# Two units to a step in the first attention, with the order of every engine written out

## The chip, the cores and the metric

The kernel runs on one core of one Trainium2 chip. The core has a matrix engine (PE, with its weight loads PEld shown apart), a vector engine (DVE), an activation engine (ACT), a general engine (POOL) and DMA queues that SP issues. PE writes its products to PSUM, a small memory of eight banks; the other engines read them from there. The metric is the device time of one execution in microseconds; smaller is better. Several executions of a kernel are taken and their median is given; one more is taken with the hardware profiler.

## The reference

The input `x` is 8 batches of 512 rows of 256 numbers. Four blocks are added to it in turn, each on the layer-normalised rows: a first attention (8 heads of 64, keys and values from a shared latent of 64), a feed-forward stack of two layers with a local attention each, a second attention (16 heads of 16, causal), and the same feed-forward stack again. The change is in the first attention:

```python
q = (x @ Wq.T).reshape(b, t, N_HEADS, HEAD_DIM)
kv_latent = x @ Wkv_down.T
k = (kv_latent @ Wk_up.T).reshape(b, t, N_HEADS, HEAD_DIM)
v = (kv_latent @ Wv_up.T).reshape(b, t, N_HEADS, HEAD_DIM)
scores = jnp.einsum('bqhd,bkhd->bhqk', q, k) * HEAD_DIM ** (-0.5)
attn = jax.nn.softmax(scores, axis=-1)
out = jnp.einsum('bhqk,bkhd->bqhd', attn, v)
out = out.reshape(b, t, N_HEADS * HEAD_DIM) @ Wo.T
...
x = L0_attn_a_x
x = x + _L0_attn_a_ref(_layernorm(x, axis=-1), ...)
x = x + _L0_ffn_ref(_layernorm(x, axis=-1), ...)
x = x + _L0_attn_b_ref(_layernorm(x, axis=-1), ...)
x = x + _L0_ffn_ref(_layernorm(x, axis=-1), ...)
```

## The kernel before

Everything is in single precision. The eight batches go through in two groups of four; each group passes all stages, so the first attention (`attention_a`) runs twice. A batch's 512 rows are four row tiles (`i`) of 128. The key and value up-projections are folded into the query and output weights at the start of a group (`fold`), so that every head's scores are a product with the 64-wide latent.

A *unit* (L377) is one batch, one row tile and two of the eight heads (`u` from 0 to 3), so a row tile is four units and a batch sixteen. A unit is five parts:

- `scores` (L381): two products `s` of 64-row operands, which lie in two halves of the array (L389); DVE's maximum of both (`nm`, L393); ACT's two exponentials with row sums (`p`, shown at L241, a helper's line).
- `divide` (L402): DVE's reciprocal of the sums (L405), ACT's two scalings of `p` in place (L407).
- `turn` (L410): eight transposes of `p` on PE into PSUM (`ppt`, L414), DVE's copy to SBUF (`pt`, L416).
- `values` (L419): sixteen products for the weighted values, as 64-column operands in the two halves of the array, into `o` (L425). With the last unit of a row tile, ACT copies `o` to `oT` (L435).
- `project` (L438): only for the last unit of a row tile: four products `pp` (L443) and DVE's addition to the residual `x` (L444).

PSUM has three tiles of two banks (`ps_s`: `s` and `ppt` share them), one of one bank (`ps_mm`: `pp` and the pieces below) and one for `o` (`ps_o`). In SBUF `p` and `pt` have three buffers each.

`prologue` (L341) prepares a batch in pieces, one to each `yield`: the layer norm on DVE and POOL (`yr`), two rounds of transposes (`pyt`, L295) with ACT copies, the latent's product (`pd`, L354) with a DVE copy, its transposes (`pl`, L360) with an ACT copy, and four query products (`pq`, L370), each with an ACT copy into `qT` (L373).

`steps` takes one unit a step, software-pipelined: in step n unit n-1 is divided, unit n gets its scores, unit n-2 is turned, n-3 weighted and n-4 projected, and one piece of the next batch's prologue is placed behind the transposes. It gives only the order of the program's text; a scheduling layer below it orders the instructions of each engine, and moves independent ones past each other. Waits are put in where data or buffers ask for them. In the other attentions that freedom is taken away by `order_keeper` (L245), which chains all instructions of an engine in the order of the text. `EARLY_STEPS` (L32) lets the next stage's first two steps begin under the end of the stage before; the last steps of the stage call `ahead` to begin the next one.

The lines of `steps` that matter here:

```python
for part in (1, 0, 2, 3, 4):
    at = step - part
    if 0 <= at < len(units):
        got[at] = units[at][part](*got.get(at, ()))
    if part == 2:
        next(pieces, None)
if step > len(units) - 6:
    ahead[0]()
```

Of the kernel before, what the change touches and what calls it, by code (L numbers as in the profile page):

```python
# [17 lines left out]
P = 128  # L18
# [20 lines left out]
GELU_TABLES = "gelu_and_others"  # L39
Piece = namedtuple("Piece", "heavy first act second dve late", defaults=(None, None, None, None, None))  # L40
Unit = namedtuple("Unit", "n product inverse error refine masks squares masked highest exponentials turn keep_turned values project")
ISSUE_ORDER = mybir.DependencyInfo(mybir.DependencyClass.NoSync, mybir.DependencyReason.DATA)
WAIT = mybir.DependencyInfo(mybir.DependencyClass.Sync, mybir.DependencyReason.SCHED_ONLY)

# [2 lines left out]
def kernel(  # L47
# [259 lines left out]
    def attention_a(batches, g):  # L307
# [69 lines left out]
        def unit(b, i, u):  # L377

            n = f"a{b}_{i}_{u}"

            def scores():  # L381
                qT, latT, lat = state[b]
                if u == 0:
                    state["sums"] = pool.tile([P, H], F32, tag="sums", name=f"sums_{n}", bufs=3)
                sums = state["sums"]
                s = ps_s.tile([P, 2, T], F32, tag="s", name=f"s_{n}")
                for odd in range(2):
                    rows = slice(odd * HD, (odd + 1) * HD)
                    nc.tensor.matmul(  # L389
                        s[:, odd], lhsT=qT[rows, u, i * P : (i + 1) * P], rhs=latT[rows, :], start=True, stop=True  # L390
                    )
                nm = pool.tile([P, 2], F32, tag="nm", name=f"nm_{n}", bufs=4)
                nc.vector.tensor_reduce(nm, s, AX.X, ALU.max, negate=True)  # L393
                p = pool.tile([P, 2, T], F32, tag="p", name=f"p_{n}", bufs=3)
                for odd in range(2):
                    h = 2 * u + odd
                    function(
                        p[:, odd], s[:, odd], AF.Exp, bias=nm[:, odd : odd + 1], accum_out=sums[:, h : h + 1]
                    )
                return p, sums, lat  # L400

            def divide(p, sums, lat):  # L402

                some = sums[:, 2 * u : 2 * u + 2]
                nc.vector.reciprocal(some, some)  # L405
                for odd in range(2):
                    nc.scalar.activation(p[:, odd], p[:, odd], AF.Identity, scale=some[:, odd : odd + 1])  # L407
                return p, lat

            def turn(p, lat):  # L410
                ppt = ps_s.tile([P, 2, NT, P], F32, tag="s", name=f"ppt_{n}")
                for odd in range(2):
                    for k in range(NT):
                        nc.tensor.transpose(ppt[:, odd, k, :], p[:, odd, k * P : (k + 1) * P], ident)  # L414
                pt = pool.tile([P, 2, NT, P], F32, tag="pt", name=f"pt_{n}", bufs=3)
                nc.vector.tensor_copy(pt, ppt)  # L416
                return pt, lat

            def values(pt, lat):  # L419
                if u == 0:  # L420
                    state["o"] = ps_o.tile([P, 4, P], F32, tag="o", name=f"o_{n}")
                o = state["o"]
                for k in range(NT):
                    for odd in range(2):
                        nc.tensor.matmul(  # L425
                            o[odd * HD : (odd + 1) * HD, u, :],
                            lhsT=lat[:, k, :],
                            rhs=pt[:, odd, k, :],
                            start=(k == 0),
                            stop=(k == NT - 1),  # L430
                        )
                if u < 3:
                    return ()
                oT = pool.tile([P, 4, P], F32, tag="two", name=f"oT_{n}", bufs=5)
                nc.scalar.copy(oT, o)  # L435
                return (oT,)

            def project(oT=None):  # L438
                if oT is None:
                    return  # L440
                pp = ps_mm.tile([P, D], F32, tag="mm", name=f"pp_{n}")
                for k in range(4):
                    nc.tensor.matmul(pp, lhsT=oT[:, k, :], rhs=wvo_a[:, k, :], start=(k == 0), stop=(k == 3))  # L443
                nc.vector.tensor_add(xs[b][:, i, :], pp, xs[b][:, i, :])  # L444

            return scores, divide, turn, values, project

        units = [unit(b, i, u) for b in batches for i in range(NT) for u in range(4)]
        each = NT * 4
        def steps(ahead):  # L450
            tables_of(EXP_TABLES)
            got, pieces = {}, iter(())
            for step in range(len(units) + 4):
                if step % each == 2 and step // each + 1 < len(batches):
                    pieces = prologue(batches[step // each + 1])
                for part in (1, 0, 2, 3, 4):
                    at = step - part
                    if 0 <= at < len(units):
                        got[at] = units[at][part](*got.get(at, ()))
                    if part == 2:  # L460
                        next(pieces, None)
                if step > len(units) - 6:
                    ahead[0]()
                yield

# [3 lines left out]
        def head():  # L469
            yield from prologue(batches[0])  # L470
            while phase["gates"]:
                yield
            for _ in range(EARLY_STEPS):
                next(rest)
                yield

        def run(ahead):
            follower.append(ahead)
# [1121 lines left out]
```

## Time and profile before

| what | value |
|---|---|
| runs | 4411.23, 4412.81, 4419.76 us; median 4412.81 us |
| span of the profiled execution | 4418.4 us |
| busy: PE, DVE, ACT, POOL | 4201.7, 3082.6, 2700.4, 1148.4 us |
| first attention, first group | first score product at 26.3 us, last one at 287.1 us |
| first attention, second group | first score product at 2219.5 us, last one at 2484.3 us |
| `s` maximum (L393), 64 in a group | 1.22 us each |
| `pt` copy (L416), 64 in a group | 1.22 us each |
| exponential of 128x512 (L241) | 0.68 us each |
| scaling of 128x512 (L407) | 0.72 us each |

The profile comes from one execution, whose span stands beside the runs' median; it is some 6 us above it. "Busy" is the time in which an engine had an instruction under way. Successive instructions of an engine overlap a little, so a step is measured from start to start. A wait is shown as idle time of an engine and what ended it. The granted clock is the share of full clock that PE had.

### The profile page before, as it was taken

To read this page: it belongs to the slowest core of one execution; us is meant where nothing else is said; L and a number is where in the kernel's file an instruction comes from. 1 tells how busy PE (TensorE), PEld (TensorE's weight loads), DVE (VectorE), ACT (ScalarE), POOL (GpSimd) and SP (SyncE) were. 2 spreads that over 40 slices of the span, in tenths; PEclk is the share of its full clock that TensorE was granted. 3 is DMA by queue.
4 is the path that set the end of the run, shared out by engine and by line. 5 is a ranking of instruction groups with operands and counts; after the bars stand their busy time and mean duration, and the time that the engine had idled before them with its cause. 6 is when DMAs were issued, how large, how long until landed. Compare 5 with 4: busy or idle time off the path is not lost.

```text
span 4418.4 us, 70438 instructions
## 1 busy us (share of the span) xinstructions
PE 4201.7 (95%) x26580; PEld 2539.8 (57%) x26580; DVE 3082.6 (70%) x7497; ACT 2700.4 (61%) x6316; POOL 1148.4 (26%) x1140
## 2 busy tenths in 40 slices
PE   9999999999998899999999999999999988999999
PEld 5666556655555465566566665565545554655655
DVE  6678737747999886377466786377479997863773
ACT  6777517716998675176167675276179886742761
POOL 0014214312222342143200242243122223422431
PEclk9999999999999999999999999999999999999999
DMA  2000000000000000000100000000000000000000
GB/s 82 1 22 4 24 3 23 3 24 20 2 1 2 20 4 7 5 21 13 53 30 1 20 4 23 22 4 23 5 21 1 1 1 20 4 6 23 3 4 24
DMA packets 51091, 63.36 MB, mean 14 GB/s; under 512 B 6336, under 2 KB 45504, under 8 KB 50752
## 3 DMA queue, kind: packets, MB, share of 16 engines
q1 hardware_dynamic: 50752, 58.85, 4.1%
q8 instruction: 211, 3.46, 0.3%
q14 instruction: 128, 1.05, 0.1%
HBM read 46.28 MB, written 4.19 MB: 11 GB/s over the span
## 4 chain that ended last, share of the span: by engine, by line
PE 74%; DVE 13%; ACT 11%; issue 1%; POOL 1%; DMA 0%; SPq 0%; POOLq 0%; ACTq 0%; DVEq 0%
PE pu_g1x L932 3%; PE pu_g0x L932 3%; PE pu_g0y L932 3%; PE pu_g1y L932 3%; PE s_a L389 3%; PE o_a L425 3%; PE ppt_a L414 3%; PE pqk_f1x L510 2%; PE pqk_f1y L510 2%; PE pqk_f0y L510 2%; PE pqk_f0x L510 2%; ACT r_b L241 2%; PE ppt_b L1269 2%; DVE pt_b L1274 2%; ACT num_b L241 2%; DVE r_b L1220 2%
## 5 line engine op out<-in xcount | busy, mean ns | idle before, releaser
L1269 PE MATMUL ppt_b<-ident,num_b 128*128 128x128 f32 x1280 | 224.1, 293 | 88.0 <-DVE pt_b L1274 63.2
L1269 PEld LDWEIGHTS ppt_b<-ident,num_b 128*128 128x128 f32 x1280 | 138.5, 144 | 273.0 <-ACT num_b L241 98.0
L241 ACT ACTIVATE num_b<-num_b,most_b 128x512 f32<-128x512 f32 (+3 forms) x512 | 280.7, 552 | 21.8 <-POOL most_b L1249 21.4
L1274 DVE COPY pt_b<-ppt_b 128x512 f32<-128x512 f32 (+1 forms) x352 | 224.1, 637 | 33.3 <-PE ppt_b L1269 32.5
L241 ACT ACTIVATE p_a<-s_a,nm_a 128x512 f32<-128x512 f32 x256 | 173.7, 683 | 105.2 <-DVE nm_a L393 102.2
L1216 DVE TENSOR_TENSOR t_b<-den_b,r_b 128x1024 f32<-128x1024 f32 (+1 forms) x176 | 197.4, 1122 | 46.3 <-ACT r_b L241 45.7
L1239 DVE CUSTOM_DVE_ANT_0 num_b<-num_b,r_b 128x512 f32<-128x512 f32 (+3 forms) x512 | 223.9, 485 | 1.9 <-POOL num_b L1232 1.9
L1232 POOL TENSOR_TENSOR num_b<-num_b,causal 128x256 f32<-128x256 f32 (+2 forms) x176 | 174.2, 990 | 186.3 <-ACT num_b L1226 185.8
L1197 PE MATMUL den_b<-st_b,st_b 18*128 18x384 f32 (+3 forms) x1024 | 210.9, 476 | 0.4 <-ACT num_b L1226 0.4
L393 DVE TENSOR_REDUCE nm_a<-s_a 128x2 f32<-128x1024 f32 x128 | 156.4, 1223 | 70.4 <-PE s_a L389 70.4
L1220 DVE SCALAR_TENSOR_TENSOR r_b<-t_b,r_b 128x1024 f32<-128x1024 f32 (+1 forms) x176 | 204.6, 1163 | 0.2
L1197 PE MATMUL dot_b<-st_b,st_b 16*128 16x384 f32 (+3 forms) x1024 | 191.4, 475 | 5.5 <-ACT yT_b L1075 4.4
L241 ACT ACTIVATE p_f1y<-p_f1y,nm_f1y,rn_f1y 128x256 f32<-128x256 f32 (+1 forms) x256 | 143.8, 564 | 80.6 <-DVE nm_f1y L649 80.5
L241 ACT ACTIVATE p_f0y<-p_f0y,nm_f0y,rn_f0y 128x256 f32<-128x256 f32 (+1 forms) x256 | 143.7, 563 | 80.6 <-DVE nm_f0y L649 80.6
L241 ACT ACTIVATE p_f1x<-p_f1x,nm_f1x,rn_f1x 128x256 f32<-128x256 f32 (+1 forms) x256 | 143.8, 564 | 75.4 <-DVE nm_f1x L649 75.3
L241 ACT ACTIVATE p_f0x<-p_f0x,nm_f0x,rn_f0x 128x256 f32<-128x256 f32 (+1 forms) x256 | 143.8, 564 | 75.2 <-DVE nm_f0x L649 75.2
L407 ACT ACTIVATE p_a<-p_a,sums_a 128x512 f32<-128x512 f32 x256 | 172.0, 720 | 26.5 <-DVE sums_a L405 26.5
L241 ACT ACTIVATE r_b<-den_b 128x1024 f32<-128x1024 f32 (+1 forms) x176 | 165.9, 942 | 33.7 <-PE den_b L1197 16.3
L1226 ACT ACTIVATE num_b<-dot_b 128x1024 f32<-128x1024 f32 (+1 forms) x176 | 164.7, 936 | 28.2 <-PE dot_b L1197 27.9
L1249 POOL TENSOR_SCALAR most_b<-most_b 128x2 f32<-128x2 f32 (+2 forms) x176 | 34.2, 194 | 568.1 <-DVE most_b L1239 552.9
L241 ACT ACTIVATE r_b<-r_b 128x1024 f32<-128x1024 f32 (+1 forms) x176 | 172.5, 980 | 5.6
L552 POOL TENSOR_TENSOR ro_f0x<-ro_f0x,rs_f0x 128x512 f32<-128x512 f32 x64 | 80.3, 1276 | 360.5 <-DVE rs_f0x L541 144.8
(356 smaller groups left out, 11296.5 us busy)
## 6 DMA issues: line engine op xcount, KB each, us to landing
x<-in_x SPq DMA_DIRECT2D x8, 512.0 KB
out<-x SPq DMA_DIRECT2D x8, 512.0 KB
wf_0x<-in_f_wqkv SPq DMA_DIRECT2D x2, 1536.0 KB
wf_0y<-in_f_wqkv SPq DMA_DIRECT2D x2, 1536.0 KB
wf_1x<-in_f_wqkv SPq DMA_DIRECT2D x2, 1536.0 KB
wf_1y<-in_f_wqkv SPq DMA_DIRECT2D x2, 1536.0 KB
wg_0x<-in_f_w SPq DMA_DIRECT2D x2, 1386.0 KB
wg_0y<-in_f_w SPq DMA_DIRECT2D x2, 1386.0 KB
```

The lines of the kernel that those rows point to most:

```text
L241: i = nc.scalar.activation(out, in_, func, **more).ins
L407: nc.scalar.activation(p[:, odd], p[:, odd], AF.Identity, scale=some[:, odd : odd + 1])
L510: nc.tensor.matmul(dst.rearrange("p h d -> p (h d)"), lhsT=hTs[b][:, k, t * P : (t + 1) * P], rhs=wqkv[:, k, c * INNER : (c + 1) * INNER], ...
L932: nc.tensor.matmul(pu[: cols.stop - cols.start, c], lhsT=w1[:, k, cols], rhs=hT[:, k, :], start=(k == 0), stop=(k == 1),)
L1197: return nc.tensor.matmul(s[:, a, m * width : (m + 1) * width], lhsT=left[at, j, past:width], rhs=right[at, j, :width], start=True, stop=True,
L1216: nc.vector.tensor_mul(t[:, :, :cols], den[:, :, :cols], r[:, :, :cols])
L1220: nc.vector.scalar_tensor_tensor(r[:, :, :cols], t[:, :, :cols], 2.0, r[:, :, :cols], ALU.subtract, ALU.mult)
L1226: nc.scalar.activation(num[:, :, :cols], dot[:, :, :cols], AF.Square, scale=-0.5)
L1232: nc.gpsimd.tensor_add(own, own, mask)
L1239: nc.vector.tensor_tensor_reduce(out=s4[:, a, m, :], in0=s4[:, a, m, :], in1=r4[:, a, m, :], scale=-1.0, scalar=LOWEST, op0=ALU.mult, op1= ...
L1269: nc.tensor.transpose(ppt[:, k, :], p[:, a, k * P : (k + 1) * P], ident)
L1274: nc.vector.tensor_copy(pt[:, a, :nblocks, :], ppt[:, :nblocks, :])
```

## The change

One step takes a *pair* of units. Every part of a unit becomes a function of its own: `scores` is now only the products, then `maxima`, `exponentials`, `invert`, `divide`, `turn`, `keep_turned`, `values`, `keep_values`, `project` and `add`. `steps` writes out their order: the products of both new units, then the weighted values of both units of two steps ago, then the maxima of the new pair, the copy `oT` where a row tile is done, the exponentials of both, and then unit by unit the transposes of the pair of one step ago with their copies, the reciprocals and the scalings. A prologue piece stands between the two turns where a row tile is done, and at the step's end otherwise; the layer norm of the next batch stands at the end of a batch's first step. All this is under `order_keeper`, so that each engine keeps the order of the text. The head of the stage takes one step (one pair) early where it took two of one unit. No buffer count changes.

```diff
         units = [unit(b, i, u) for b in batches for i in range(NT) for u in range(4)]
-        each = NT * 4
+        pairs = [units[at : at + 2] for at in range(0, len(units), 2)]
+        each = NT * 2
+
         def steps(ahead):
             tables_of(EXP_TABLES)
-            got, pieces = {}, iter(())
-            for step in range(len(units) + 4):
-                if step % each == 2 and step // each + 1 < len(batches):
-                    pieces = prologue(batches[step // each + 1])
-                for part in (1, 0, 2, 3, 4):
-                    at = step - part
-                    if 0 <= at < len(units):
-                        got[at] = units[at][part](*got.get(at, ()))
-                    if part == 2:
+            kept_order = order_keeper()
+            pieces = iter(())
+
+            def pair(m):
+                return pairs[m] if 0 <= m < len(pairs) else ()
+
+            for m in range(len(pairs) + 2):
+                new, turning, weighted = pair(m), pair(m - 1), pair(m - 2)
+                done = weighted[1] if weighted and m % 2 else None
+                with kept_order():
+                    for some in new:
+                        some.scores()
+                    for some in weighted:
+                        some.values()
+                    for some in new:
+                        some.maxima()
+                    if done:
+                        done.keep_values()
+                    for some in new:
+                        some.exponentials()
+                    if turning:
+                        turning[0].turn()
+                        turning[0].keep_turned()
+                    if new:
+                        new[0].invert()
+                    if done:
                         next(pieces, None)
-                if step > len(units) - 6:
+                    if new:
+                        new[0].divide()
+                    if turning:
+                        turning[1].turn()
+                        turning[1].keep_turned()
+                    if new:
+                        new[1].invert()
+                        new[1].divide()
+                    if done:
+                        done.project()
+                        done.add()
+                    else:
+                        next(pieces, None)
+                    if m % each == 0 and m // each + 1 < len(batches):
+                        pieces = prologue(batches[m // each + 1])
+                        next(pieces)
+                if m > len(pairs) - 3:
+                    ahead[0]()
                     ahead[0]()
                 yield
...
-            for _ in range(EARLY_STEPS):
-                next(rest)
-                yield
+            next(rest)
+            yield
```

Inside `unit`, the parts are the same instructions as before, split into these functions; what a part hands to the next stands in a dictionary `got` of the unit.

## The prediction

> **What bounds the kernel now.** I read the page's busy shares first, then the chain that ended last, then the windows cut at the batches of the first attention, then TensorE's order of time inside one of them, and last the waits. A "quad" below is four units (one row tile), a "pair" two.
>
> Of the page, the first line shows the busiest engine, the second what the end of the span hangs on:
>
> ```profile
> PE 4201.7 (95%) x26580; PEld 2539.8 (57%) x26580; DVE 3082.6 (70%) x7497; ACT 2700.4 (61%) x6316; POOL 1148.4 (26%) x1140
> ...
> PE 74%; DVE 13%; ACT 11%; issue 1%; POOL 1%; DMA 0%; SPq 0%; POOLq 0%; ACTq 0%; DVEq 0%
> ```
>
> Both are averages over stages. The windows (start:end, length, then busy time of PE, PEld, DVE, ACT, POOL, then granted clock) show the first attention's second and third batch and three quads of its fourth, and below them a stretch of the second attention for the clock:
>
> ```profile
> 93.40:160.50 67.10, 67.10 (x513) 42.45 (x512) 47.24 (x69) 49.10 (x108) 1.46 (x3) 1.00 0.00 1
> 160.50:227.70 67.20, 67.20 (x515) 42.49 (x514) 43.71 (x57) 49.20 (x108) 1.21 (x2) 1.00 0.00 1
> 227.70:270.70 43.00, 43.00 (x361) 28.40 (x360) 31.54 (x39) 34.32 (x76) 0.00 (x0) 1.00 0.02 4
> 1300.00:1400.00 100.00, 92.03 (x828) 51.52 (x826) 90.34 (x196) 87.03 (x171) 21.51 (x40) 0.93 0.01 1
> ```
>
> In the first attention PE has no gap at all: other engines have a third to spare. So only fewer PE microseconds can shorten this stage, and any wait that PE gets lengthens it. One quad and the beginning of the next, in PE's order of time (start, length, instruction):
>
> ```profile
> 213.31 1.13 PE L389 MATMUL s_a<-latT_a,qT_a 64*128 64x512 f32 x4
> 214.37 1.09 PE L414 MATMUL ppt_a<-ident,p_a 128*128 128x128 f32 x8
> 215.39 1.09 PE L425 MATMUL o_a<-pt_a,lat_a 128*64 128x128 f32 x16
> 216.41 1.13 PE L389 MATMUL s_a<-latT_a,qT_a 64*128 64x512 f32 x4
> ...
> 225.73 1.99 PE L443 MATMUL pp_a<-wa,oT_a 128*128 128x256 f32 x8
> 227.66 1.13 PE L389 MATMUL s_a<-latT_a,qT_a 64*128 64x512 f32 x4
> ```
>
> From start to start: s 1.06, ppt 1.02, o 1.02, pp 1.93; a quad is 227.66 - 213.31 = 14.35 us. Elsewhere ppt takes 0.93 when a product of its own array shape follows (204.51 to 205.44, then pq), so each change of shape costs about 0.09 at the end of one, and two s in a row took
>
> ```profile
> 2219.47 1.99 PE L389 MATMUL s_a<-latT_a,qT_a 64*128 64x512 f32 x8
> 2221.29 0.38 PE L961 MATMUL po_g0y_mm<-wg_0y,gT_g0y 42*128 42x256 f32 x1
> ```
>
> 1.82 us against 2 x 1.06; with a change of shape behind them 1.91.
>
> **What the change saves on PE.** s,s 1.91 for 2.12; o,o and (where nothing comes between) ppt,ppt have no row: at most 2.04 (nothing saved), at least 1.86 (2 x 0.93); I take 1.90. Per pair 0.21 + 0.14 + 0.14 = 0.49, per quad 0.98, over 32 quads (two groups of four batches of four) 31 us. That would be the gain with PE still full. No product, transpose, DMA or ACT pass is added or dropped. EARLY_STEPS for this attention goes from two units to one pair, the same work.
>
> **What the fixed order adds.** Three PSUM buffers serve s, s, ppt, ppt. In the changed kernel's allocation, a step's first s takes the buffer of the step before's first ppt, its second s that of the second s before, its second ppt that of its own first s. So PE waits (1) at the first s for the copy pt of the first ppt one step back, (2) at the second ppt for the first unit's exponentials. Behind (1) everything on PE waits, behind (2) the projection too; neither was a wait before, since each unit's chain had a unit's time for itself. On ACT, in steps that finish a quad, the copy oT stands ahead of the exponentials, and so waits for the second o.
>
> Latencies, from rows: ppt's start to its copy's start 1.08 (299.07 to 300.15), copy 1.22, a DVE end to PE's start 0.14:
>
> ```profile
> 44.19 1.22 DVE L416 COPY pt_a<-ppt_a 128x1024 f32<-128x1024 f32 x1
> ...
> 45.55 0.52 PE L414 MATMUL ppt_a<-ident,p_a 128*128 128x128 f32 x3 [0.58 <-DVE pt_a L416]
> ```
>
> *Step without a finished quad*: s,s 0 to 1.91, o,o to 3.81, first ppt 3.81, its copy 4.89 to 6.11, next s at 6.25. PE alone would need 1.91 + 1.90 + 1.90 = 5.7: 0.55 of wait. (DVE is free at 3.3: two maxima of 1.12 from 1.06 on.)
>
> *Step with one*: second o starts at 2.78; o's start to oT's 1.14 (303.76 to 304.90): 3.92; oT holds ACT 0.47 (156.18 to 156.65); exponentials of unit one 4.39 to 5.85 (first one's start to the reciprocal's wait end, 148.63 to 150.11, less 0.03); second ppt 5.99, pp 6.92 (0.93), next s 8.7 (1.8: like pq 205.44 to 207.25). PE alone 5.7 + 1.8 = 7.5: 1.2 of wait.
>
> Together 14.95 for a quad against 14.35: **the two waits (1.75) eat the 0.98 and more, +0.6 per quad without other work.** With hand-overs between engines at nothing it would be 5.9 + 8.3 = 14.2 (0.87 of transposes, then the copy; ACT's two passes, then pp); with each of the six 0.1 longer, 15.55.
>
> **Where the next batch's preparation fills the waits.** It is eight pieces of PE work; before, they cost PE 67.1 - 4 x 14.35 = 9.7 us a batch. Afterwards: in a finishing step they lie between the two ppt, in the 1.2 us hole. pd (1.7) makes it 9.3, pq (its ACT copy must free the one mm buffer before pp) 9.65; in a plain step pyt and pl (0.4 to 0.6) hide wholly, pq gives 7.4 (5.55 + 1.71 + 0.1). Against that, two new stalls at a batch's start: the layer norm is in DVE's fixed order (statistics 1.75, 11.46 to 13.21; POOL 1.4 to 14.59; rows 1.38), ahead of the next maxima, and the last qT copy stands behind both divisions on ACT, so the second s waits 1.1. The step after it takes 11.1. Steps of one batch: 7.4, 11.1, 6.25, 9.3, 6.25, 9.65, 7.4, 9.65 = 67.0, against 67.1: no change in two of four batches.
>
> *First batch.* From its unit 4 on, 48.5 to unit 16 (6.25, 9.3, 6.25, 9.65, 7.4, 9.65), against 53.1 (40.3 to 93.4). But in the first group unit 4 starts later: maximum of unit 1 ends about 34.6, its exponentials 36.1, then on DVE the layer norm (4.6), a maximum (1.1), the rotation tables (2.77, which stood at 40.31 before) and a maximum, then the copy: s of unit 4 at 47.1 instead of 40.3. Net +2.2. In the second group the layer norm lies under the feed-forward's last products (2221 to 2231): unit 4 at 2236.9 for 2237.6, net -5.2.
>
> *Last batch.* Steps 7.4, 9.8, then 6.25 and 8.7 twice = 47.1 for 43.05: +4.05. The tail, to the end of the last pp, interleaved with the next stage's start: before 36.8 us (270.7 to 307.5); after 39.3, since two of pht, hT, pqk and of POOL's sum, pqt leave some 3 us of PE holes where 1.3 stood. +2.5.
>
> Sum: group one 2.2 - 0.2 + 4.05 + 2.5 = +8.5; group two -5.2 - 0.2 + 4.05 + 2.5 = +1.1; **+9.6 us on the profiled 4418.4 = 4428.0.** That execution lies 5.6 above the runs' median of 4412.81, so the runs should read about **4422.5**, +0.22%. The two groups' whole stage is some 560 us; the rest of the kernel keeps its order.
>
> What about the clock: it was granted 1.00 here and 0.93 in the stretch of the second attention above, where PE is 92% busy and turns much by transposes. In the new quads PE will be 89% busy (14.35 - 0.98 of 14.95), and between the last o and pp lie 3.3 us with only transposes. I take no loss from it; the rival below prices one.
>
> [...]
>
> **Rivals.**
> *PE stays full* (not slower): the waits are hidden because some hand-over is shorter or ACT runs ahead. It holds if the copy ends before 5.6 and the exponentials before 4.6 of their steps. For it: DVE and ACT are idle a third. Against it: both waits are chains of latency, not of load. 4412.8 - 31 = 4382; half hidden 4398 to 4402.
> *The clock drops* (slower than forecast): holes and transposes bring the 0.93 of that stretch here. On half of the stage's 560 us PE loses 280 x 0.07 = 20, of which the holes hide perhaps a quarter: 4437. For it: the stretch's busy share is like the new one. Against it: no window of this stage is under 1.00. It decides from a granted clock of 0.97 over the stage.
> *It does little, within 0.2%*: the same mechanism, with a per-quad price of +0.4 instead of +0.6, gives 32 x -0.2 = -6: 4416.
>
> **How the numbers follow.** My mechanism 0.65 (own range 4412 to 4434: per-quad error of 0.3 over 32 quads), two fifths of it inside 0.2% (8.8 us, about what a measurement of this kernel can tell from no change: 4404 to 4421.6), PE full or nearly 0.2, clock 0.15. Slower 0.65 x 0.6 + 0.13 = 0.52; faster 0.2; same 0.65 x 0.4 + 0.02 = 0.28. The range reaches down to half-hidden waits and up to the clock's case: 4396 to 4440, leaving about 0.12 below and 0.07 above.
>
> **What will show it.** Right: PE's idle before s_a put down to pt_a some 0.5 us in every second step, before ppt_a to the exponentials p_a about 1.2 in the others; starts of s pairs 6.25 and 8.7 apart in the last batch; s,s 1.91; a batch near 67. Wrong: s pairs at 5.7 and 7.5 (PE full), a granted clock under 1.00 in the windows, a layer norm that runs elsewhere on DVE, or a time shift in stages that the change does not touch.

## The result, and the profile after

| | before | after |
|---|---|---|
| median of 4 runs | 4414.36 us | 4432.69 us |
| ratio, 95% interval | | 1.004 [1.0026, 1.0054] |
| span of the profiled execution | 4418.4 us | 4430.5 us |
| first attention, group one | 288.63 us | 300.16 us |
| first attention, group two | 292.64 us | 296.01 us |
| PE busy in both groups | 574.6 us | 554.6 us |
| PE idle in both groups | 6.7 us | 41.6 us |

The changed kernel is 0.4% slower. The two stage lengths run from the first score product of a group to the first weighted values of the next stage, read from TensorE's order of time; from here on "the stages" are both together. They grew by 11.5 and 3.4, together 14.9 us; the medians differ by 18.3. Of the 14.9, PE's work fell by 20.0 us, and its idle time rose by 34.9.

The page's first line and its chain answer to the two shown of before:

```profile
PE 4175.9 (94%) x26580; PEld 2547.3 (57%) x26580; DVE 3073.0 (69%) x7497; ACT 2690.1 (61%) x6316; POOL 1147.7 (26%) x1140
...
PE 72%; DVE 14%; ACT 12%; issue 1%; POOL 1%; DMA 0%; SPq 0%; POOLq 0%; ACTq 0%; DVEq 0%
```

PE is busy 26 us less and the span is 12 us longer; two per cent of the chain went from PE to DVE and ACT. The windows of the changed kernel, cut at the second batch, the third batch, the hole at the start of group one and the end of the third batch's first finishing step (columns as before):

```profile
96.85:164.14 67.29, 64.07 (x513) 43.43 (x513) 44.67 (x65) 47.69 (x108) 1.20 (x2) 1.00 0.00 1
164.14:233.78 69.64, 65.51 (x513) 44.35 (x513) 48.73 (x85) 47.69 (x108) 3.75 (x7) 0.98 0.00 1
...
36.00:48.30 12.30, 4.11 (x22) 3.26 (x20) 9.65 (x26) 6.10 (x15) 1.21 (x2) 0.72 0.00 0
...
182.00:185.25 3.25, 3.05 (x9) 2.25 (x9) 2.42 (x7) 2.59 (x5) 0.00 (x0) 0.62 0.00 0
```

Before, the second batch took 67.10 us with PE busy for all of it. Now it takes 67.29 with PE busy for 64.07: three microseconds of work are saved and three of waiting put in their place. The third batch is 2.4 us longer than before, and in two places the granted clock is far under 1.00. One quad of the last batch, and the beginning of the next, in PE's order of time (L numbers are now lines of the changed kernel):

```profile
257.23 1.99 PE L393 MATMUL s_a<-latT_a,qT_a 64*128 64x512 f32 x8 [0.44 <-DVE pt_a L430]
259.15 1.97 PE L439 MATMUL o_a<-pt_a,lat_a 128*64 128x128 f32 x32
261.05 1.09 PE L426 MATMUL ppt_a<-ident,p_a 128*128 128x128 f32 x8
263.15 1.09 PE L426 MATMUL ppt_a<-ident,p_a 128*128 128x128 f32 x8 [1.01 <-ACT p_a L244]
264.08 1.89 PE L455 MATMUL pp_a<-wa,oT_a 128*128 128x256 f32 x8
265.90 1.99 PE L393 MATMUL s_a<-latT_a,qT_a 64*128 64x512 f32 x8
...
272.13 1.13 PE L393 MATMUL s_a<-latT_a,qT_a 64*128 64x512 f32 x4 [0.44 <-DVE pt_a L430]
```

From start to start, the scores of a pair (s,s) take 1.92 and its weighted values (o,o) 1.90; a finishing step, one in which a row tile's projection is done, takes 8.67 (257.23 to 265.90), a plain one 6.23 (265.90 to 272.13). The two waits stand where the prediction put them: 0.44 us at the first score product for the copy `pt`, 1.01 us at the second turn for the exponentials. Steps of the changed kernel, in microseconds from one pair's first score product to the next ("behind the layer norm", below also "layer norm step", is the step after the one at whose end the next batch's layer norm stands):

| step | forecast | measured |
|---|---|---|
| plain | 6.25 | 6.22 |
| finishing a quad | 8.7 | 8.67 |
| plain, with a query product | 7.4 | 7.43 |
| finishing, with `pd` | 9.3 | 9.34 |
| finishing, with a query product | 9.65 | 9.66 |
| behind the layer norm, second batch | 11.1 | 11.32, 11.33 |
| behind the layer norm, third batch | 11.1 | 13.68, 13.18 |
| a batch with pieces, second / third | 67.0 | 67.29, 67.30 / 69.64, 69.14 |
| start of unit 4 in group one | 47.1 | 48.31 (the stage began 0.94 later) |

### The profile page after: what moved, and what is told of

Same layout as the page of the kernel before. It is cut to its first block, busy times and chain, and to the rows that moved or that the text cites. A ratio compares the mean times of both kernels' runs of the same rounds, so it can differ in the third digit from the quotient of the medians.

```text
span 4430.5 us, 70536 instructions
## 1 busy us (share of the span) xinstructions
PE 4175.9 (94%) x26580; PEld 2547.3 (57%) x26580; DVE 3073.0 (69%) x7497; ACT 2690.1 (61%) x6316; POOL 1147.7 (26%) x1140
## 3 DMA queue, kind: packets, MB, share of 16 engines
q14 instruction: 128, 1.05, 0.1%
## 4 chain that ended last, share of the span: by engine, by line
PE 72%; DVE 14%; ACT 12%; issue 1%; POOL 1%; DMA 0%; SPq 0%; POOLq 0%; ACTq 0%; DVEq 0%
PE pu_g1x L983 3%; PE pu_g0x L983 3%; PE pu_g0y L983 3%; PE pu_g1y L983 3%; PE o_a L439 3%; PE s_a L393 3%; PE pqk_f0y L561 2%; PE pqk_f1y L561 2%; PE pqk_f0x L561 2%; PE pqk_f1x L561 2%; ACT r_b L244 2%; PE ppt_a L426 2%; PE ppt_b L1320 2%; DVE pt_b L1325 2%; ACT num_b L244 2%; DVE r_b L1271 2%
## 5 line engine op out<-in xcount | busy, mean ns | idle before, releaser
L244 ACT ACTIVATE num_b<-num_b,most_b 128x512 f32<-128x512 f32 (+3 forms) x512 | 280.7, 552 | 20.2 <-POOL most_b L1300 19.8
L430 DVE COPY pt_a<-ppt_a 128x1024 f32<-128x1024 f32 x128 | 155.7, 1219 | 106.3 <-PE ppt_a L426 106.3
L1277 ACT ACTIVATE num_b<-dot_b 128x1024 f32<-128x1024 f32 (+1 forms) x176 | 164.6, 935 | 27.7 <-PE dot_b L1248 27.6
L603 POOL TENSOR_TENSOR ro_f1x<-ro_f1x,rs_f1x 128x512 f32<-128x512 f32 x64 | 80.4, 1278 | 363.0 <-DVE rs_f1x L592 149.7
```

The lines of the kernel that those rows point to most:

```text
L244: i = nc.scalar.activation(out, in_, func, **more).ins
L430: nc.vector.tensor_copy(got["pt"], got.pop("ppt"))
L1277: nc.scalar.activation(num[:, :, :cols], dot[:, :, :cols], AF.Square, scale=-0.5)
```

## The experiments

Each version was timed beside the kernel before, whose medians were 4416.0, 4418.6 and 4415.1 us in the three series. "Stages" is the difference to before in the two stage lengths together, "PE" the difference in PE's busy time inside them, "idle" PE's idle time there, "half clock" the time inside them for which the record of the granted clock stands at 0.5; all are from the profiled execution. e3_between, e5_keep_later and e6_single_kept were executed five times, the other experiments eleven; the profiled execution of e3_between lies 11.6 us under its median and that of e2_ln_free 7.8 us, so for these two the stages and the medians need not agree.

| version | median us | ratio, interval | stages | PE | idle | half clock |
|---|---|---|---|---|---|---|
| before | | | 0 | 0 | 6.7 | 0 |
| changed | 4432.69 | 1.0040 [1.0026, 1.0054] | +14.9 | -20.0 | 41.6 | 13.7 |
| e1_free | 4417.53 | 1.0007 [0.9999, 1.0016] | +2.2 | -21.3 | 30.2 | 3.4 |
| e2_ln_free | 4425.97 | 1.0022 [1.0013, 1.0031] | +8.9 | -23.2 | 38.7 | 0 |
| e3_between | 4433.96 | 1.0039 [1.0024, 1.0054] | +12.4 | -12.8 | 31.8 | 20.5 |
| e4_both | 4407.42 | 0.9984 [0.9975, 0.9993] | -5.7 | -19.8 | 20.7 | 3.4 |
| e5_keep_later | 4438.04 | 1.0055 [1.0041, 1.0069] | +19.0 | -16.1 | 41.8 | 23.9 |
| e6_single_kept | 4457.18 | 1.0088 [1.0074, 1.0102] | +42.6 | +18.0 | 31.3 | 34.1 |
| e7_between_free | 4426.44 | 1.0015 [1.0007, 1.0024] | +10.7 | +3.9 | 13.4 | 0 |
| e8_more_p | 4420.37 | 1.0011 [1.0002, 1.0020] | +8.3 | -20.0 | 34.9 | 23.9 |
| e10_single_ln_free | 4416.94 | 1.0004 [0.9995, 1.0013] | +5.1 | +0.8 | 10.9 | 0 |
| e11_both_ahead | 4409.59 | 0.9989 [0.9980, 0.9998] | -9.8 | -20.5 | 17.4 | 0 |
| e12_ln_free_keep_between | 4404.48 | 0.9978 [0.9969, 0.9986] | -8.9 | -27.9 | 25.7 | 0 |
| e13_keep_between | 4421.35 | 1.0014 [1.0005, 1.0023] | +7.1 | -19.5 | 33.2 | 23.9 |

### What the fixed order costs: e1_free, e2_ln_free

```diff
-            kept_order = order_keeper()
+            kept_order = nullcontext
```

> The changed kernel without the fixed order: the text keeps its pairs, each engine's order is free. TensorE's order and the allocation of the three PSUM tiles stay those of pairs; what moves are the layer norm and some copies on DVE and ACT. Theory A (the hand-over of PSUM tiles inside a step sets the time, the layer norm in its fixed place adds to it): quads of the last batch stay near 14.9 us, the finishing step a little shorter if ACT takes oT later; the layer norm steps fall from 11.3 and 13.7 to about 9.3 us and the hole of 15 us at the start of group one shrinks by some 6 us; time 4405 to 4420. Theory B (the loss of freedom itself costs, pairs alone would gain): quads of 13.3 us or less and a time of 4382 to 4400.

The time is that of theory A, and theory B's falls: pairs without the fixed order are as fast as before, not faster. But a quad of the last batch takes 13.66 us, nearer to B's 13.3 than to A's 14.9, since the finishing step is 7.44: the free order puts `oT` behind the first unit's exponentials, between its two scalings, which A had down as "a little shorter". In exchange a finishing step with `pd` takes 10.1 to 10.9 us, and 15.2 in the first batch of group two; in the second batch PE is idle for 1.5 us of it before `pp_a`.

In e2_ln_free only the layer norm is outside:

```diff
-                    if m % each == 0 and m // each + 1 < len(batches):
-                        pieces = prologue(batches[m // each + 1])
-                        next(pieces)
+                if m % each == 0 and m // each + 1 < len(batches):
+                    pieces = prologue(batches[m // each + 1])
+                    next(pieces)
```

> The changed kernel, with only the next batch's layer norm taken out of the fixed order. Theory A: the plain and finishing steps stay 6.22 and 8.67 us; the steps of 11.3 (second batches) and 13.7 and 13.2 us (third batches) become about 9.3, and unit 4 of group one starts near 41 to 42 us instead of 48.3: 6.8 + 2 + 4.4 + 2 + 3.9 = 19 us less than the changed kernel, about 4414. Theory B' (the place of the layer norm costs nothing, another engine is late there): no change, 4430 to 4435.

Unit 4 of group one starts at 42.51 instead of 48.31, the layer norm steps of group one are 10.77 us instead of 11.32 and 13.68; plain and finishing steps stay 6.22 and 8.67. The direction is A's, the size a third of it: 6.0 us instead of 19. The steps don't come down to 9.3, because PE still waits three times in them: 0.84 us at the second score product for the last query copy, 0.58 at the second turn for the exponentials, and 0.72 at `pp_a`, which needs the PSUM tile of the transposed rows, whose copy stands on ACT behind the exponentials.

What "outside" means shows on DVE: the rows `yr` of the third batch are normalised from 50.5 to 53.0 us, and their first transpose follows at 105.2, so that nothing waits for them. It isn't free everywhere. The first batch of group one is 5.2 us shorter than in the changed kernel and the third batches 2.9 and 2.4, but the second batches are 0.7 us longer each (the step behind the layer norm step grows from 6.22 to 7.48; on DVE, rows of the next stage now stand between the maxima), and the first batch of group two is 3.2 us longer: there statistics of the layer norm stand ahead of a copy `pt` on DVE and wait 3.83 us for the transfer of `x`, and PE waits 2.45 us for that copy.

The third batch of the changed kernel shows why the layer norm is dearer there. Its first finishing step in time, all engines (start, length, instruction, idle before it and what ended it), and below it two lines of the same step of the second batch:

```profile
174.71 0.41 DVE L279 BATCH_NORM_STATS2 st_f0x<-x 128x6 f32<-128x256 f32 x1
...
176.34 1.38 DVE L286 TENSOR_SCALAR yr_a<-x,mv_a,rstd_a 128x256 f32<-128x256 f32 x4 [1.22 <-POOL rstd_a L270]
...
177.63 2.35 DVE L399 TENSOR_REDUCE nm_a<-s_a 128x2 f32<-128x1024 f32 x2
178.88 0.69 ACT L244 ACTIVATE p_a<-s_a,nm_a 128x512 f32<-128x512 f32 x1 [1.68 <-DVE nm_a L399]
...
180.39 1.34 PE L426 MATMUL ppt_a<-ident,p_a 128*128 128x128 f32 x8 [2.28 <-ACT p_a L244]
...
182.20 3.12 PE L455 MATMUL pp_a<-wa,oT_a 128*128 128x256 f32 x8 [0.47 <-ACT yT_a L352]
...
111.87 1.09 PE L426 MATMUL ppt_a<-ident,p_a 128*128 128x128 f32 x8 [1.12 <-ACT p_a L244]
113.68 1.99 PE L455 MATMUL pp_a<-wa,oT_a 128*128 128x256 f32 x8 [0.72 <-ACT yT_a L352]
```

The scores were there from 174.7 on, but DVE takes their maxima only at 177.63, behind the normalised rows `yr_a`. Those are late since statistics of the *next* stage (`st_f0x`, for a batch that is done) slip in between this batch's own, as its `rstd` does on POOL: nothing holds them back, as the fixed order of the first attention covers only its own instructions. From the step's first score product to the maxima it is 6.06 us, against 4.83 in the second batch. So PE waits 2.28 us here, against 1.12. And then its projection takes 3.12 us instead of 1.99: the window 182.00 to 185.25 above has a granted clock of 0.62. Of the 2.36 us that this step is longer, half is wait and half is work at the lower clock. The stretch of half clock lasts from 181.09 to 184.50 and begins 0.7 us after the hole, around which PE did hardly more than transposes (o,o until 176.5, then `ppt`, `pyt`, the hole, `ppt`). Whether the hole brought it, or the transposes, or both, no run here shows.

### The two hand-overs: e3_between, e5_keep_later, e8_more_p, e13_keep_between

e3_between puts other TensorE work in front of both waits:

```diff
-                    for some in weighted:
-                        some.values()
                     for some in new:
                         some.maxima()
-                    if done:
-                        done.keep_values()
-                    for some in new:
-                        some.exponentials()
                     if turning:
                         turning[0].turn()
                         turning[0].keep_turned()
+                    for some in weighted:
+                        some.values()
+                    for some in new:
+                        some.exponentials()
+                    if done:
+                        done.keep_values()
```

> The changed kernel with the weighted values of both units put between the two turns, and the copy oT behind the exponentials: s, s, ppt, o, o, ppt. Both PSUM hand-overs then have 2 to 3 us of other TensorE work before them, for one more change of array shape (0.09 us) a step. Theory A: plain step 5.8 to 5.9 us, finishing step 7.6 to 7.7 us, quad 13.5, last batch's three quads 40.6 instead of 44.7; no idle time of TensorE before s_a or ppt_a there; time 4400 to 4415 with the layer norm still in its place. Theory C (the saving of array shape changes isn't there, or ACT is the bound of a step): steps stay at 6.2 and 8.7, time 4428 or more.

PE in the last batch:

```profile
255.60 1.99 PE L393 MATMUL s_a<-latT_a,qT_a 64*128 64x512 f32 x8
257.51 1.09 PE L426 MATMUL ppt_a<-ident,p_a 128*128 128x128 f32 x8
258.54 1.97 PE L439 MATMUL o_a<-pt_a,lat_a 128*64 128x128 f32 x32
260.43 1.09 PE L426 MATMUL ppt_a<-ident,p_a 128*128 128x128 f32 x8
261.56 1.99 PE L455 MATMUL pp_a<-wa,oT_a 128*128 128x256 f32 x8
263.49 1.99 PE L393 MATMUL s_a<-latT_a,qT_a 64*128 64x512 f32 x8
```

No line has an idle time: the steps are 7.89 (255.60 to 263.49) and 5.86, theory A's to 0.2 us, and theory C falls. Yet the time is no better than the changed kernel's. The expectation had counted on a saving in every batch. But the second batches still take 67.5 us, and the third ones 71.3 and 70.8, longer than the 69.6 and 69.1 of the changed kernel: there the prologue's pieces had filled the hole already, as the prediction had said, and the layer norm step stands at 11.48 in the second batch and at 14.50 in the third. So where pieces lie, the hand-overs were worth little, and the layer norm holds the gain.

e5_keep_later moves only `oT`, behind both units' exponentials, and e8_more_p also takes every second unit's `p` from another ring of three buffers:

```diff
-                    if done:
-                        done.keep_values()
                     for some in new:
                         some.exponentials()
+                    if done:
+                        done.keep_values()
```

```diff
-                got["p"] = p = pool.tile([P, 2, T], F32, tag="p", name=f"p_{n}", bufs=3)
+                got["p"] = p = pool.tile([P, 2, T], F32, tag="ro" if u % 2 else "p", name=f"p_{n}", bufs=3)
```

> The changed kernel with one thing moved: in a step that finishes a quad ACT takes the copy oT behind the exponentials instead of ahead of them. Theory A: the wait of 1.01 us before the second turn goes, since the first unit's exponentials begin about 1.9 us earlier; finishing step 7.5 us instead of 8.67 where nothing of the prologue lies in it, 9.2 instead of 9.66 with a query product; plain steps stay 6.22 us with their 0.44 us wait; sum about 14 us less than the changed kernel, 4418. Rival (the projection then waits for oT as long as the turn did for the exponentials): finishing step stays 8.5 or more, time 4430 or more.

> The changed kernel with oT behind the exponentials (that alone took 8.89 us a finishing step, with 1.0 us of wait of the second unit's exponentials and 1.19 us of TensorE for oT), and the second unit's exponentials p taken from another ring of three buffers, so that they needn't wait for the first turn of the same step. Theory A (it was the p buffer that held them): no idle of ACT between the two units' exponentials, finishing step 7.5 us; the PSUM tiles come round in another order, the first score product no longer after the copy pt, so the plain step 5.8 to 6.2 us; quads 13.3 to 13.7; layer norm steps stay over 11; 4410 to 4420. Rival (ACT's own work holds oT): finishing step stays 8.5 or more, 4432 or more.

The rival's case came: a finishing step of e5_keep_later takes 8.89 us. ACT and PE there:

```profile
263.80 1.97 PE L426 MATMUL ppt_a<-ident,p_a 128*128 128x128 f32 x16
264.98 0.69 ACT L244 ACTIVATE p_a<-s_a,nm_a 128x512 f32<-128x512 f32 x1 [1.00 <-ACT p_a L244]
...
266.32 0.58 ACT L449 COPY oT_a<-o_a 128x512 f32<-128x512 f32 x1
...
266.95 1.99 PE L455 MATMUL pp_a<-wa,oT_a 128*128 128x256 f32 x8 [1.19 <-ACT oT_a L449]
```

The second unit's exponentials wait 1.00 us, `oT` behind them, and the projection for `oT`. The releaser named there is ACT itself, which had been free since 264.0; the wait that counts is for the first of the two turns on the line above it, the last reader of the `p` buffer that they write into (three buffers, two units a step). e8_more_p shows it: with the other ring the four exponentials follow each other without a gap (260.99 to 263.6). The edit also brings the PSUM tiles round in another order, so that no plain step waits (5.71 us). Its finishing step is 8.24, not 7.5, because PE still waits for `oT` at the end of ACT's row:

```profile
264.28 1.99 PE L455 MATMUL pp_a<-wa,oT_a 128*128 128x256 f32 x8 [0.54 <-ACT oT_a L449]
```

So the mechanism of A holds and its size was too large; `p` with three buffers is a third hand-over, which the prediction didn't have.

e13_keep_between puts `oT` into that very gap of ACT:

```diff
-                    if done:
-                        done.keep_values()
-                    for some in new:
-                        some.exponentials()
+                    if new:
+                        new[0].exponentials()
+                    if done:
+                        done.keep_values()
+                    if new:
+                        new[1].exponentials()
```

> The changed kernel with one statement moved: oT between the exponentials of the two units instead of ahead of both. Theory A: finishing step 7.4 to 7.6 us instead of 8.67, 9.2 instead of 9.66 with a query product, layer norm steps still 11 to 14 us; some 12 to 15 us below the changed kernel: 4418 to 4422. Rival (oT ahead of the exponentials is not what holds the second turn): finishing step stays 8.67, 4430 or more.

```profile
259.65 1.97 PE L426 MATMUL ppt_a<-ident,p_a 128*128 128x128 f32 x16
259.76 0.58 ACT L449 COPY oT_a<-o_a 128x512 f32<-128x512 f32 x1
260.83 0.69 ACT L244 ACTIVATE p_a<-s_a,nm_a 128x512 f32<-128x512 f32 x1 [0.48 <-PE ppt_a L426]
261.45 1.89 PE L455 MATMUL pp_a<-wa,oT_a 128*128 128x256 f32 x8
```

Both turns now run as one (x16), the projection follows without a wait, and the step takes 7.44 us instead of 8.67; with a query product 9.23 instead of 9.66. ACT's wait is named after PE's turn, as argued for e5_keep_later. The time, 4421.4, is in A's interval, although the layer norm steps grew to 13.4 and 14.8 us in group one (11.8 and 14.8 in group two), with 23.9 us of half clock.

Two of the waits that repeat are for a buffer: PE's 0.44 us in each plain step without a piece, for a PSUM tile, and ACT's 1.00 us in e5_keep_later, for a `p`. But the longer of PE's two repeated gaps in the changed kernel, 1.01 us in a finishing step without a piece, went without another buffer, by one copy's place.

### Fixed order with single units: e6_single_kept, e10_single_ln_free

```diff
+            kept_order = order_keeper()
...
-                for part in (1, 0, 2, 3, 4):
...
+                with kept_order():
+                    for part in (1, 0, 2, 3, 4):
...
```

In e10_single_ln_free, the layer norm is issued outside of it, which also brings every later piece one step forward:

```diff
                     pieces = prologue(batches[step // each + 1])
+                    next(pieces)
```

> The kernel before, one unit a step, with its steps put under the fixed order and nothing else. Theory A (a fixed order costs by itself, through the layer norm and the tables in front of the maxima): quads stay 14.35 us, TensorE idle 2 to 4 us at each layer norm and some 5 at the start of group one: 10 to 15 us over before, 4426 to 4431. Rival (only pairs suffer under it, a single unit's step has slack): within 4 us of before, 4412 to 4420.

> One unit a step under the fixed order (that cost 42.6 us in the two stages), with the layer norm outside of it. Its layer norm steps stood at 10.6 and 13.6 us where 3.5 would do, and one step at the start of group one at 12.2; these are some 40 us of the 42.6. Theory A (the fixed order costs nothing but the place of the layer norm): the stages come back to within 6 us of before, 4414 to 4424. Rival (the fixed order of ACT and TensorE costs too): 15 us or more remain, 4433 or more.

The quads stay 14.35 us, and the cost is at the layer norm, as A says, but at 42.6 us it is three to four times A's size. One layer norm step of e6_single_kept:

```profile
115.28 1.38 DVE L283 TENSOR_SCALAR yr_a<-x,mv_a,rstd_a 128x256 f32<-128x256 f32 x4 [1.41 <-POOL rstd_a L267]
115.75 1.30 PE L295 MATMUL pyt_a<-ident,yr_a 128*128 128x128 f32 x4 [2.28 <-DVE yr_a L283]
...
116.65 1.21 DVE L393 TENSOR_REDUCE nm_a<-s_a 128x2 f32<-128x1024 f32 x1
...
119.96 1.99 PE L443 MATMUL pp_a<-wa,oT_a 128*128 128x256 f32 x8 [1.90 <-ACT yT_a L349]
```

Here the transposes of the rows follow in the same step, so that PE waits 2.28 us for the rows themselves and 1.90 us more for their copy; the step is 10.6 us long, where the one with these transposes takes 3.5 in e10_single_ln_free (the one behind it, at 6.3, has a wait of 0.80). With the layer norm free, 37.5 of the 42.6 us are gone: 20.4 us of PE's waits, and 17.2 us of its busy time, which at 34.1 us of half clock against none is the same work done more slowly. So the place of the layer norm, with the clock that comes with it, is nearly all that the fixed order costs a single unit (the pieces' one step forward was not tried by itself). Under the same fixed order, with the layer norm in it, pairs are 27.7 us faster than single units (+14.9 against +42.6): PE's busy time is 38.0 us less, by the saved changes of shape and less half clock (13.7 against 34.1), and it waits 10.3 us more.

### Versions that beat both: e4_both, e12_ln_free_keep_between, e11_both_ahead; and e7_between_free

e4_both joins e2_ln_free and e3_between; e11_both_ahead is that with the next stage begun a step earlier; e12_ln_free_keep_between joins e2_ln_free and e13_keep_between; e7_between_free is e3_between without the fixed order. The one new line is that of e11_both_ahead:

```diff
-                if m > len(pairs) - 3:
+                if m > len(pairs) - 4:
```

> Both earlier edits together: the weighted values between the two turns (with oT behind the exponentials), and the layer norm outside the fixed order. Alone, the first gave steps of 5.86 and 7.9 us where no prologue lies and saved nothing where it does, because the layer norm's step stood at 11.5 and 14.5 us; alone, the second took 6.4 us out of the two stages. Theory A (with the PSUM waits gone, the layer norm's place is all that holds TensorE): layer norm steps of 8.5 to 9.5 us, batches with pieces of 64 to 65.5 us instead of 67.3, about 15 to 22 us below the changed kernel's 4432.7: 4410 to 4418, or below. Rival (another chain of the batch's start takes its place: the copy of the transposed rows, or that of the last query product): batches stay at 66.5 or more, 4420 to 4426.

> The changed kernel with the layer norm outside the fixed order and the copy oT put between the exponentials of the two units, where ACT waits 1.0 us for the p buffer in any case; weighted values stay in their place. Theory A (the second hand-over is oT's place, nothing else): finishing step 7.4 to 7.6 us, with a query product 9.2; plain step still 6.22 with 0.44 of wait; some 12 to 15 us below the version with the free layer norm alone: 4410 to 4414. Rival (the projection then waits for oT, as with oT behind both exponentials): finishing step 8.5 or more, 4424 or more.

> The version with the weighted values between the turns and a free layer norm (4407 us), with the next stage begun one step earlier (two more calls). Its tail, from unit 60 to the next stage's first score product, is some 3 us longer than before's in each group, with TensorE idle 1.47, 0.52, 0.78 and 0.67 us. Theory A (the tail lacks work to put into those holes): 2 to 3 us less a group, 4401 to 4404. Rival (the next stage's copies stand in front of the attention's own on DVE and ACT): no change or up to 4 us more, 4406 to 4412.

> The weighted values between the two turns in the text, no fixed order. Theory A (pairs gain once neither the hand-overs nor the layer norm hold TensorE): steps of 5.9 and 7.5 to 7.9 us, batches with pieces 64 to 65.5 us, 4400 to 4408, below before. Rival (the free order puts copies and scalings late, as in the pairs without the fixed order where steps with pieces kept 1.5 us of waits): 4412 to 4420, no gain over before.

e4_both and e12_ln_free_keep_between are faster than before, and e12_ln_free_keep_between is better than expected; each needs both of its edits. In e4_both the layer norm steps are 8.81 us, as in A; the second and third batches, at 66.0 and 64.8, stand on either side of A's upper bound of 65.5. In e12_ln_free_keep_between the stages are 17.8 us below those of e2_ln_free, where A had 12 to 15. Alone, its two edits gave 6.0 (e2_ln_free) and 7.8 us (e13_keep_between), together 23.8. Half of what it has over e13_keep_between alone, 8.4 of 16.0 us, is PE's busy time, with no half clock where that had 23.9 us. Its second batch and one quad of the last:

```profile
91.19:157.62 66.43, 63.67 (x514) 43.43 (x513) 46.34 (x69) 48.20 (x108) 1.20 (x2) 1.00 0.00 1
238.78:252.45 13.67, 13.23 (x121) 9.70 (x121) 10.08 (x13) 11.09 (x26) 0.00 (x0) 1.00 0.00 1
```

A quad is 13.67 us against 14.35 of before, and the saving of PE in both groups, undisturbed by half clock, is 27.9 us. Of these, 19.0 go back as idle time (25.7 against 6.7): in each layer norm step 0.84 at the second score product and 0.75 at `pp_a`, 0.44 in each plain step of the last batch, and the rest mostly at the start and the end of a group.

e11_both_ahead has 4.1 us less in the stages than e4_both, of them 1.7 in the tail of each group, where its theory A said 2 to 3; its median, 4409.6, is in the rival's range and doesn't show it. The intervals of the three overlap, and which is fastest stays open.

e7_between_free did neither of what was expected: PE is idle for only 13.4 us, but busy 24 us more than in e4_both. A plain step's scores there, and the beginning of a finishing step:

```profile
252.06 1.99 PE L393 MATMUL s_a<-latT_a,qT_a 64*128 64x512 f32 x8
...
257.92 1.12 PE L393 MATMUL s_a<-latT_a,qT_a 64*128 64x512 f32 x2
258.97 1.99 PE L455 MATMUL pp_a<-wa,oT_a 128*128 128x256 f32 x8
```

A unit's two score products are four instructions, and lie in the two halves of the array. The free order puts the projection between the two of the next pair's first unit: the first product alone (x2) takes 1.05 us from start to start, as long as both together before (x4, 1.06), and the other six instructions, from 260.90 to 262.81, take as long as all eight in a plain step, 1.92. So a finishing step is 8.83 us instead of the 7.90 of e4_both. This stands in 22 of the 32 row tiles, and 22 x 0.93 us are 20 of the 24. It is the work side by side in the two halves that is lost here, more than changes of shape.

## Why the prediction came out as it did

*What bounds the stage: right.* PE had no gap, other engines had a third to spare. The versions that take PE's waits away and keep its saving (e4_both, e12_ln_free_keep_between) shorten the stages; e7_between_free, which waits least of all pairs but has PE busy for longer, doesn't.

*The saving: right.* s,s was taken as 1.91 and measured 1.92, o,o as 1.90 and measured 1.90. The 31 us over both groups show as 27.9 in e12_ln_free_keep_between. PE alone was put at 5.7 and 7.5 us a step; without waits a plain step takes 5.71 (e8_more_p) and a finishing step 7.44 (e13_keep_between).

*The two waits: right in place, releaser and size* (steps of 6.25 and 8.7 forecast, 6.22 and 8.67 measured; idle times of 0.55 and 1.2 forecast, 0.44 and 1.01 shown); e3_between takes both away, e13_keep_between the second. The prediction saw that `oT` stands ahead of the exponentials, but counted the turn's wait for them as the price of the pair; e13_keep_between shows it to be the price of that place. *PE stays full* falls for the changed kernel, and so does *it does little*.

*Where the preparation fills the waits: right for the second batch, and this is the step that failed for the third.* "The step after it takes 11.1" was worked out once and taken for every batch; in the third it measured 13.68 and 13.18 us. The forecast counted this stage's own layer norm on DVE, but not the next stage's, which is outside the fixed order and falls into the same place (1.16 us more of wait), nor the half clock that follows the longer hole (about as much again). Batches two and three were forecast to cost -0.2 us a group; they cost +2.7 and +2.2.

*The first and the last batch: right; the tail: too large.* First batch +2.5 for +2.2 in group one, -5.2 for -5.2 in group two; last batch +4.0 for +4.05. The tail is what remains: 11.5 - 2.5 - 2.7 - 4.0 = +2.3 in group one and 3.4 + 5.2 - 2.2 - 4.0 = +2.4 in group two, for +2.5 each. That agreement is in part luck: the forecast's tail ended with the last `pp_a`, and to there it is 38.3 us for 36.8 of before, +1.5, with 1.6 us of PE's holes where some 3 were forecast; the rest comes behind it.

*The sum:* 9.6 us forecast, 14.9 measured in the stages; 5.1 of the 5.3 between them are the four layer norm steps (0.2, 2.6, 0.2 and 2.1 over 11.1). The median came 10.2 us above the forecast's 4422.5, well inside a range (4396 to 4440) that ran from half-hidden waits to the clock's case. Besides these 5.3, 1.6 are the median of before, which rose from 4412.81 to 4414.36 with a fourth execution. The remaining 3.3 are not explained: outside the stages the profiled execution of the changed kernel was 2.8 us shorter, not longer, than that of before. The 5.6 that the forecast took off is a span set against a device time; in the changed kernel's profiled execution the two differ by 1.8 (4430.5 and 4432.33). That doesn't touch the forecast, which is the median of before plus 9.6.

*The clock drops:* the lower clock is real, the price was put on the wrong thing. It isn't the mixture of holes and transposes in each step, for the quads of the last batch have a granted clock of 1.00; it came in three stretches, 13.7 us together, at the start of group one and in the third batches, so that over the stages the clock was 0.99, not the rival's 0.97. (The transposes and the wait between o and pp, put at 3.3 us, are 3.1 by the prediction's own terms and 3.03 in the quad above.) Versions with the layer norm in the fixed order have 13.7 to 34 us of it, those without 0 to 3.4. The stretch that begins at 41.14 us does so 2.16 us into a gap of 5.94 us, in the window with PE busy for 4.11 of 12.30; the one in the third batch of group one begins 0.7 us behind a gap of 2.28 with transposes on either side of it, and that of group two 0.3 us before the end of such a gap of 2.29. The length of a gap alone doesn't decide it: in the second attention of the kernel before, PE has two gaps of 3.04 us, with the same instructions just before them and in the 1.98 us behind them; the one that ends at 1479.15 us is followed by a stretch of 3.41 us from 1481.14 on, and in the 8.95 us behind the one that ends at 3673.55 the granted clock is 1.00. What brings a stretch, no run here shows.

## What to carry to other kernels

When an order is fixed by hand, look for the long chain that has no due time (here a layer norm of 5 us on DVE with a detour through POOL) and try it outside: in single units its place was 37.5 of the 42.6 us that the order cost. In pairs freeing it gave 6.0 us, less than moving one copy (7.8), and the two together 23.8; so edits of this kind are tried together as well as alone. When parts are gathered to save an engine's changes of shape (27.9 us of PE's work in e12_ln_free_keep_between), follow each buffer's ring through the new order first: what was hidden by alternation became a wait here (0.44 us at the first score product, 1.01 at the second turn), and moving one copy into a gap of its own engine can be worth as much as a buffer (e13_keep_between and e8_more_p, +7.1 and +8.3 us in the stages). A step that is worked out for one batch must be worked out again where the next stage's work begins to fall into it.

## What the runs showed of the hardware

The parts of the kernel that no version touches differ between profiled executions by as much as some of these edits are worth: the span from the first group's attention to the second's was 5.3 us shorter in the profile of the changed kernel than in that of before, with 20.5 us at half clock in it against 37.5, and over all versions it is 1.8 to 7.6 us shorter. A difference of a few microseconds is therefore read from the length of the stage that was changed, where a plain step came out at 6.22 or 6.23 us in every version that left it alone, and only then from the medians.

Two products of 64 rows in the two halves of the array take as long as one of them alone: 1.06 and 1.05 us (e7_between_free). In the stages of the changed kernel the three stretches at half clock lasted 6.827, 3.413 and 3.413 us, and the half clock of every version in the table of the experiments (3.4, 13.7, 20.5, 23.9 and 34.1 us) is to a tenth a multiple of 3.413.
